# Bank ticks on VectorE, a first pass shared 3:1, and rearranged borders, in a two-layer convolution kernel

## The chip, the cores and the metric

The kernel runs on one core of a Trainium2 chip. The metric is the device time of one execution in microseconds (us). The engines are called as the profile calls them: PE is TensorE's matmul side and PEld its weight loads, DVE is VectorE, ACT is ScalarE, POOL is GpSimd, SP is SyncE, which here only issues DMAs. "L506" is line 506 of the kernel before.

## The reference

The input x is (4, 64, 256, 256) in float32: four images of 64 channels. Two residual layers follow each other, `x = x + layer(groupnorm(x))`, with 32 groups.

```python
# layer 0
h = gelu(conv3x3(gn(x), c1_w) + c1_b)
xa, k = split(conv1x1(h, c2_w) + c2_b)
xs = gelu(conv_3x1(conv_1x3(xa, sh_w), sv_w))          # depthwise
mask = top2(softmax(mean(xs) @ gate_w.T))              # per image, 3 experts
out = xs + sum(e_w3 @ ((e_w2 @ k) * (e_w1 @ xs)) * mask_e)   # ranks 2, 4, 8
x = x + conv1x1(out, proj_w)
# layer 1
g = gn(x)
h = relu(batchnorm(conv3x3(g, quantize(w1)) + b1))
h = batchnorm(conv3x3(h, quantize(w2)) + b2)
x = x + relu(h + g)
```

GroupNorm needs statistics of a whole image before its first convolution, BatchNorm statistics of the whole batch.

## The kernel before

**Stages.** There are six, one after the other. (1) The first pass loads image 0 in 16 chunks of 1 MB (`stats_load`) and takes its statistics. (2) The front works through 64 units of 16 image rows, 16 units to an image: layer 0 up to the gate. Statistics of the next image, and the closing part of layer 0 for the last one (experts, projection, residual, stored to `y_d`), are laced into it. (3) conv1 is layer 1's first convolution; its result goes to `h_d`. (4) The BatchNorm sums are closed (`totals_close`, `bn_affine`), which holds up conv2. (5) conv2 goes over 64 chunks of `h`; the last chunks stay on the chip, 50 go to memory. (6) The end loads `y` (and the 50 `h`) again, applies BatchNorm, both residuals and ReLU, and stores `out`.

**First pass.** DVE takes statistics of 512 elements with `bn_stats` (`stats_group`, L415); ACT takes a piece of 1024 elements with two activations with sums, Identity and Square (`stats_piece`, L444). `stats_parts` gives half of the chunks' elements to each: 32 groups and 16 pieces. `stats_end` joins them: `bn_aggr` over all groups (L475), the sums of ACT's pieces (`stats_sums`, L446), then `combine` (L267–L284), which averages over the channels of a group with two small matmuls. `scale_weights` (L458) multiplies the convolution's weights by the reciprocal deviation, giving `us`; for image 0 in four parts on DVE (L465), for the others on ACT (L467).

**A unit of the front.** The 3x3 convolution is a short Winograd form over rows. POOL makes the transformed inputs: `x_fourths` (L546), `x_seconds` (L554), `v_inner` and `v_outer` (L580–L589), for the next two units. PE multiplies in three groups into two banks `ps_c`: products (1,2), (3,4), then (0,5). ACT copies one half of each bank (`front_copy`, L619), DVE combines (`butterfly_a` to `butterfly_d`, L624–L643), ACT applies GELU (`front_h`, L651). `butterfly_c` (L636, L637) writes into the bank that products (0,5) add to. Then follow the taps of the separable convolutions: `front_taps_a` is 24 matmuls into a bank `ps_a`, `front_taps_b` 8 more into the same bank, for the rows from neighbouring units; ACT (`front_taps_i`, L692) and DVE (`front_taps_h`, L699, L707, L710) finish the horizontal taps, ACT the GELU (L723). This is done twice in a unit, for sub 1 of unit u−2 and for sub 0 of unit u−1.

**Ticks.** Between `front_taps_a` and `front_taps_b` stands `divide` (L497). It writes one column with a memset that waits for the last matmul before it, and the first matmul behind it waits for the memset:

```python
ins = nc.gpsimd.memset(tick, 0.0)
tc.add_manual_dep(ins.ins, last[0].ins.name, finished, reason="bank change")
```

There are two ticks in a unit, at positions 2.2 and 7.2; both are on POOL.

**The order of the work.** It is written out by hand. `at_slot(u, pos, call)` puts a step into slot u; positions under 6 belong to its first half and the others to its second, and steps are emitted sorted by half and position. All five engines keep the order in which instructions are emitted, so an instruction that waits holds up all that stands behind it on its engine. Steps that take several visits, such as `stats_end`, `out_end` and the scaling of layer 1's weights (`weights1_scale`, `weights1`, L253–L255 among its lines), are generators: each visit in the plan runs one of their parts.

**conv1 and conv2.** A convolution over a chunk of 8 rows works on even and odd rows apart. `differences` (L343) and `upper_odd`/`lower_odd` (L359 on ACT, L362 on DVE) prepare the inputs, PE multiplies (L296), DVE writes the result with the sums (L318), and `square` (L382, ACT) takes the sums of squares for BatchNorm. In conv2, `conv2_affine` (L1295) first applies BatchNorm and ReLU to the loaded chunk.

**The end.** For each chunk: load y (L1441), `v = gn2_scale * y + shift` on ACT (L1453), `h = scale * h + v` on DVE (L1454), `h = max(h, 0) + y` on DVE (L1455), store (L1456). SP issues loads and stores in order; nine y loads are issued ahead (AHEAD = 8 and one in the loop), into 3 old tiles and MORE = 6 new ones.

## Time and profile before

| | |
|---|---|
| median of 3 runs | 2990.66 us (2983.44 to 2991.94) |
| the profiled execution | 2990.48 us, its span 2988.7 us |
| PE busy, share of the span | 2351.9 us, 79% |
| DVE | 2440.1 us, 82% |
| ACT | 2024.8 us, 68% |
| POOL | 1682.5 us, 56% |
| bytes moved by DMA | 915.33 MB, 306 GB/s over the span |

The span runs from the first to the last instruction on the chip; 1.8 us of the execution lie outside it. A row of a timeline gives the start and the length in us, the engine, the line, the operation, what it writes and reads, how many follow each other as one row (x3), and in brackets the idle time before it with what ended it. A row of the waits gives the waiting engine and line, the instruction it waited for, the sum in us, how often, and the longest. A row of the stages gives the stretch, its length, the busy time of PE, PEld, DVE, ACT and POOL (with the number of instructions), the granted clock of PE, the busy share of the DMA engines and GB/s. Busy shares are means over stages with different limits, so they say little alone.

### The profile page before, as it was taken

The numbers are of one execution on the slowest core, as the hardware profiler recorded it, in microseconds if no ns is written. First come the engines' busy times: TensorE is split into PE (matmuls) and PEld (weight loads), VectorE is DVE, ScalarE is ACT, GpSimd is POOL, SyncE is SP. The second block draws the span as 40 slices with busy tenths as digits, with TensorE's granted clock in tenths as the row PEclk, the third lists the DMA queues.
The fourth block names the chain that finished last, engine by engine and source line by source line (L and its number), as shares of the span: only waits on it lengthen the run. The fifth ranks groups of instructions, "written<-read, shape, count | busy, mean of one in ns | idle before, by whom it ended". The sixth has DMA issues, their size and how long they took to land.

```text
span 2988.7 us, 52829 instructions
## 1 busy us (share of the span) xinstructions
PE 2351.9 (79%) x21576; PEld 1500.3 (50%) x21576; DVE 2440.1 (82%) x2754; ACT 2024.8 (68%) x2210; POOL 1682.5 (56%) x1283
## 2 busy tenths in 40 slices
PE   1888899999999999989999999989999999100000
PEld 1444445444444555546666667867888888000000
DVE  5678678878878888868988889979999898876665
ACT  6777888778776665567666667968888888432222
POOL 5888888778778888734544546735555565000000
PEclk9999999999999999999999999989999999555555
DMA  8565579999999899849999997747777763899999
GB/s 348 206 237 209 196 270 370 357 350 353 345 336 321 295 320 323 293 181 323 361 345 358 340 337 275 283 164 269 262 266 263 264 234 140 354 420 425 425 424 407
DMA packets 135570, 915.33 MB, mean 306 GB/s; under 512 B 14944, under 2 KB 15712, under 8 KB 40608
## 3 DMA queue, kind: packets, MB, share of 16 engines
q1 hardware_dynamic: 107680, 777.74, 70.1%
q10 hardware_dynamic: 27648, 134.23, 11.3%
q8 instruction: 169, 2.77, 0.4%
q14 instruction: 73, 0.60, 0.1%
HBM read 573.74 MB, written 338.17 MB: 305 GB/s over the span
## 4 chain that ended last, share of the span: by engine, by line
PE 50%; DMA 27%; DVE 10%; POOL 6%; ACT 3%; issue 3%; SPq 0%; ACTq 0%; DVEq 0%; POOLq 0%
PE ps_h L296 19%; PE ps_c L506 8%; PE ps_a L506 6%; PE ps_h2m L296 6%; DMA y<-in_xp 6%; DMA y_d<-y 5%; PE ps_o L506 5%; DMA y_end<-y_d 5%; DMA out<-h 4%; DMA h<-h_d 4%; PE ps_hm L296 3%; POOL x L554 2%; DMA xs_in<-xs_d 2%; DVE y L873 1%; DVE t L707 1%
## 5 line engine op out<-in xcount | busy, mean ns | idle before, releaser
L296 PE MATMUL ps_h<-diff,w_q 128*128 128x512 f32 x3072 | 756.8, 401 | 17.6 <-DVE h L318 17.2
L296 PEld LDWEIGHTS ps_h<-diff,w_q 128*128 128x128 f32 x3072 | 578.9, 190 | 196.1 <-issue 28.8
L506 PE MATMUL ps_c<-v,us 64*64 64x256 f32 x9216 | 538.4, 382 | 28.6 <-DVE ps_c L637 23.8
L343 POOL TENSOR_TENSOR d<-yn 128x1024 f32<-128x1024 f32 x128 | 347.8, 2738 | 305.6 <-DMA yn<-y_d 189.8
L506 PEld LDWEIGHTS ps_c<-v,us 64*64 64x64 f32 x9216 | 359.3, 135 | 180.5 <-DVE ps_c L637 24.2
L506 PE MATMUL ps_a<-h,av 64*64 64x512 f32 x4080 | 388.0, 494 | 55.2 <-DVE t L710 40.1
L343 POOL TENSOR_TENSOR d<-h 128x1024 f32<-128x1024 f32 x127 | 311.9, 2478 | 194.8 <-DVE diff L351 133.3
L318 DVE SCALAR_TENSOR_TENSOR h<-ps_h,scale_w,m 128x1024 f32<-128x1024 f32 x256 | 322.8, 1279 | 73.3 <-PE ps_h L296 53.4
L554 POOL TENSOR_TENSOR x<-x 128x512 f32<-128x512 f32 x256 | 330.0, 1289 | 12.5
L1453 ACT ACTIVATE v<-y_end,shift,gn 128x2048 f32<-128x2048 f32 x64 | 133.8, 2093 | 280.2 <-DMA y_end<-y_d 245.1
L506 PEld LDWEIGHTS ps_a<-h,av 64*64 64x64 f32 x4080 | 153.8, 133 | 331.6 <-issue 203.5
L382 ACT ACTIVATE junk<-h,less_h 128x2048 bf16<-128x2048 f32 (+3 forms) x133 | 255.9, 1924 | 11.1 <-DVE h L318 10.9
L1454 DVE SCALAR_TENSOR_TENSOR h<-h,ss,v 128x2048 f32<-128x2048 f32 x64 | 149.8, 2349 | 121.4 <-ACT v L1453 96.8
L692 ACT ACTIVATE t<-ps_a,tap_bias,m 128x1016 f32<-128x1016 f32 x128 | 153.4, 1199 | 128.7 <-PE ps_a L506 99.7
L873 DVE SCALAR_TENSOR_TENSOR y<-ps_o,ob,y 128x1024 f32<-128x1024 f32 x128 | 163.9, 1280 | 74.8 <-PE ps_o L506 26.8
L723 ACT ACTIVATE xs<-t 128x1024 f32<-128x1024 f32 x128 | 134.8, 1053 | 102.3 <-DVE t L710 88.4
L296 PE MATMUL ps_h2m<-odd,w_q 128*128 128x512 f32 x768 | 193.2, 401 | 8.2 <-DVE odd L362 4.4
L296 PE MATMUL ps_hm<-odd,w_q 128*128 128x512 f32 x768 | 191.4, 398 | 2.8 <-DVE t L710 1.3
L353 DVE SCALAR_TENSOR_TENSOR diff<-d,gn,diff 128x1024 fp32r<-128x1024 f32 x128 | 192.3, 1531 | 0.5 <-ACT diff L346 0.5
L346 ACT ACTIVATE diff<-d 128x1024 fp32r<-128x1024 f32 x128 | 135.1, 1056 | 83.3 <-POOL d L343 82.1
L546 POOL TENSOR_TENSOR x<-x,x 128x512 f32<-128x512 f32 x128 | 160.9, 1280 | 22.2 <-ACT x L540 22.2
L296 PEld LDWEIGHTS ps_h2m<-odd,w_q 128*128 128x128 f32 x768 | 146.3, 191 | 44.5 <-DVE odd L362 5.2
(250 smaller groups left out, 4271.5 us busy)
## 6 DMA issues: line engine op xcount, KB each, us to landing
x<-in_xc SPq DMA_DIRECT2D x64, 1280.0 KB
h<-h_d SPq DMA_DIRECT2D x64, 1152.0 KB
yn<-y_d SPq DMA_DIRECT2D x60, 1152.0 KB
xs_in<-in_xp SPq DMA_DIRECT2D x64, 1024.0 KB
xs_d<-xs ACTq DMA_DIRECT2D x128, 512.0 KB
xs_in<-xs_d SPq DMA_DIRECT2D x64, 1024.0 KB
y<-in_xp SPq DMA_DIRECT2D x64, 1024.0 KB
y_d<-y SPq DMA_DIRECT2D x64, 1024.0 KB
```

The costliest lines, as they stand in the source:

```text
L296: nc.tensor.matmul(ps, wq[w][:, kind, kx, :], t[:, rows, kx : kx + W], start=(j == 0), stop=(j == len(terms) - 1))
L318: nc.vector.scalar_tensor_tensor(h.rearrange("p (e k) w -> p e (k w)", e=2), ps.rearrange("p e k w -> p e (k w)"), w_scale[w], m.unsqueeze ...
L343: engine.tensor_tensor(raw.rearrange("p (g r) w -> p g r w", g=2), *pair, ALU.subtract)
L346: nc.scalar.activation(inner(tiles[0], 4 * n, 4 * n + 4), raw, AF.Copy, scale=scale)
L353: nc.vector.scalar_tensor_tensor(lower, raw, scale, upper.bitcast(F32), ALU.mult, ALU.subtract)
L382: nc.scalar.activation(junk[rows, 0:n], flat(h), AF.Square, bias=less[name][rows], accum_out=total)
L506: last[:] = [nc.tensor.matmul(ps[o, at_out[0] : at_out[1], :], w[i], rhs[i], **flags)]
L546: nc.gpsimd.tensor_tensor(x4[:, j - 1], x_rows(u, j + 2), x4[:, j - 1], ALU.subtract)
L554: nc.gpsimd.tensor_tensor(x[:, r : r + 2], x[:, r + 2 : r + 4], x[:, r : r + 2], ALU.subtract)
L692: nc.scalar.activation(t[:, :, inside], ps[:, :, inside], AF.Identity, bias=tap_bias, scale=sh[:, 1:2])
L873: nc.vector.scalar_tensor_tensor(y, ps.rearrange("p x s w -> p x (s w)"), out_bias[b], y, ALU.add, ALU.add)
L1454: nc.vector.scalar_tensor_tensor(h, h, ss2[:, 0:1], v, ALU.mult, ALU.add)
```

## The change

- `divide` takes the unit. In slots under 16 it writes its tick with a memset on DVE, into a column of its own; elsewhere with POOL as before. These are 29 of the 128 ticks: sub 1 in slots 2 to 15 and sub 0 in slots 1 to 15.
- In the first pass every second chunk, and chunk 14, is split between DVE (two groups) and ACT (one piece); the others, chunk 15 among them, are DVE's whole: 48 groups and 8 pieces. Every 16 groups, `bn_aggr` joins them into a column of `mv_x`, and `combine` gets four columns in place of two. `scale_weights` is on ACT for image 0 too.
- DVE's steps of the weights of layer 1 go from position 6.2 to 7.3, and its second stats groups for image 1 from 6.2 to 7.25, both behind the tick at 7.2.
- Two chain steps go later: one of `stats_end` from (e+2, 6.15) to (e+2, 8.3), the first of `out_end` from (e+1, 4.1) to (e+1, 8.35).
- The square of conv1's last chunk is taken in two halves, the first ahead of the chunk's last output.
- For conv2's first chunk, DVE applies BatchNorm and ReLU to the even rows and the last one, and both first differences are DVE's; ACT's `upper_odd` stands straight behind its odd rows. The odd tiles are allocated ahead of the difference tiles.
- In the end the formula is turned round: DVE `h * inverse + y`, ACT `Relu(gn2_scale * h + shift)`, DVE `h + y`. Part of `inverse` and `shift` is made in conv2, at chunk 8 (`end_scales`, eight one-column operations). The first chunk goes in two halves. MORE is 8, AHEAD is 10, the v tiles are gone, and the order on SP, DVE and ACT is written out.

The diff (lines without a mark are context, "..." stands for lines left out):

```diff
     def stats_group(b, g, k, i):
         if g == 0:
-            st_g[b] = lstat.tile([P, NG // 2, 6], F32, tag="st_x", name=f"st_x{b}", bufs=1)
+            st_g[b] = lstat.tile([P, 3 * NG // 4, 6], F32, tag="st_x", name=f"st_x{b}", bufs=1)
...
+    def stats_join(b, i, n):
+        nc.vector.bn_aggr(mv_x[b][:, 1 + i, :], flat(st_g[b][:, i * n : i * n + n, :]))
+    mv_x = {}
+    PARTS = (4, 2, 1, 1)
...
     def stats_shift(b):
...
-    HALVED = (0, 1)
     def stats_parts(k):
...
     def stats_sums(b, mv):
...
-        n = NCH if b in HALVED else 2 * NCH
+        n = 2 * NCH // PARTS[b]
...
         for a, e in parts:
...
-            if b == 0:
-                nc.vector.tensor_scalar(o, u, gn1[b][:, 1:2], None, ALU.mult)
-            else:
-                nc.scalar.activation(o, u, AF.Copy, scale=gn1[b][:, 1:2])
+            nc.scalar.activation(o, u, AF.Copy, scale=gn1[b][:, 1:2])
+    def stats_open(b):
+        n = PARTS[b]
+        mv_x[b] = stat.tile([P, n, 2], F32, tag=f"mv{n}", name=f"mv_x{b}")
...
     def stats_end(b):
...
-        n = 2 if b in HALVED else 1
-        mv = stat.tile([P, n, 2], F32, tag=f"mv{n}", name=f"mv_x{b}")
-        if b in HALVED:
-            nc.vector.bn_aggr(mv[:, 1, :], flat(st_g.pop(b)))
+        n = PARTS[b]
+        if b > 0:
+            stats_open(b)
+        if n == 2:
+            stats_join(b, 0, NG // 2)
+        mv = mv_x.pop(b)
...
-    tick = column("tick")
+    tick, tick_v = column("tick"), column("tick_v")
...
-    def divide():
-        ins = nc.gpsimd.memset(tick, 0.0)
+    def divide(u):
+        ins = nc.vector.memset(tick_v, 0.0) if u < NCH else nc.gpsimd.memset(tick, 0.0)
...
         if g:
...
-    def conv1_square(b, k):
+    def conv1_square(b, k, part=None):
+        if part is not None:
+            h = h_out[b, k][:, 4 * part : 4 * part + 4, :]
+            square("h1", h, junks[0], squares[b][:, k + 2 * part : k + 2 * part + 1])
+            if part:
+                nc.scalar.dma_start(h1_d[b][:, k * CPAIR : (k + 1) * CPAIR, :], h_out.pop((b, k)))
+            return
...
         if k == 0:
...
+        stats_open(0)
+        groups = pieces = 0
         for k in range(NCH):
...
             if k == 0:
...
-            groups, pieces = stats_parts(k)
-            for group in groups:
-                stats_group(0, *group)
-            for n, at_sum in pieces:
+            both_engines = k % 2 == 1 and k < NCH - 1 or k == NCH - 2
+            for i in range(2 if both_engines else 4):
+                stats_group(0, groups, k, i)
+                groups += 1
+                if groups % (NG // 4) == 0:
+                    stats_join(0, groups // (NG // 4) - 1, NG // 4)
+            if both_engines:
                 for i in range(2):
-                    stats_piece(0, n, i, at_sum)
+                    stats_piece(0, 2 * k + 1, i, pieces)
+                pieces += 1
             if k == 5:
...
             if k == 8:
...
             if 0 <= u - 2 <= last:
...
-                at_slot(u, 2.2, divide)
+                at_slot(u, 2.2, divide, u)
...
             if 0 <= u - 1 <= last:
...
-                at_slot(u, 7.2, divide)
+                at_slot(u, 7.2, divide, u)
...
-        at_slot(3, 6.2, weights1_top)
+        at_slot(3, 7.3, weights1_top)
...
-        at_slot(4, 6.2, next, chain, None)
+        at_slot(4, 7.3, next, chain, None)
         for i, name in enumerate(("w1", "w2")):
...
             for n in range(3):
-                at_slot(7 + 3 * i + n, 6.2, next, chain, None)
+                at_slot(7 + 3 * i + n, 7.3, next, chain, None)
...
     def plan_stats(b):
...
             if k == 0:
...
-            groups, pieces = stats_parts(k) if b in HALVED else ([], [(2 * k, None), (2 * k + 1, None)])
+            groups, pieces = stats_parts(k) if PARTS[b] == 2 else ([], [(2 * k, None), (2 * k + 1, None)])
             for i, (n, at_sum) in enumerate(pieces):
...
             for group in groups:
...
-                at_slot(int(s), 4.1 if s - int(s) < 0.5 else 6.2, stats_group, b, *group)
+                at_slot(int(s), 4.1 if s - int(s) < 0.5 else 7.25, stats_group, b, *group)
...
-        places = (e, 8.3), (e + 1, 1.25), (e + 1, 1.36), (e + 2, 1.25), (e + 2, 1.36), (e + 2, 4.45), (e + 2, 6.15), (e + 3, 1.25), (e + 3, 1.36)
+        places = (e, 8.3), (e + 1, 1.25), (e + 1, 1.36), (e + 2, 1.25), (e + 2, 1.36), (e + 2, 4.45), (e + 2, 8.3), (e + 3, 1.25), (e + 3, 1.36)
...
         for place in places:
...
         if count == NOCT:
...
-            for place in ((e + 1, 4.1), (e + 2, 1.25), (e + 2, 1.36), (e + 3, 1.25), (e + 3, 1.36), (e + 3, 4.45), (e + 3, 8.3)):
+            for place in ((e + 1, 8.35), (e + 2, 1.25), (e + 2, 1.36), (e + 3, 1.25), (e + 3, 1.36), (e + 3, 4.45), (e + 3, 8.3)):
...
     def plan_out_late(b, ns, steps, order, end):
...
-            at(T + 4 + 4 / 3, 13.16, conv1_square, b, k)
+            if (b, k) == (B - 1, NCH - 1):
+                at(T + 4, 12.85, conv1_square, b, k, 0)
+                at(T + 4, 12.92, conv1_square, b, k, 1)
+            else:
+                at(T + 4 + 4 / 3, 13.16, conv1_square, b, k)
...
+    def conv2_affine_vector(i):
+        (even, _), _ = second_rows(h_in[i])
+        for rows in (even, h_in[i][:, CPAIR, :]):
+            nc.vector.tensor_scalar(rows, rows, ss1[:, 0:1], ss1[:, 1:2], ALU.mult, ALU.add)
+            nc.vector.tensor_scalar(rows, rows, 0.0, None, ALU.max)
+        nc.vector.memset(h_in[i][C:P, 0, :], 0.0)
     def conv2_affine(i, part=None):
...
-    diffs2 = [difference_tiles(halves_pool, f"2{i}", 6, CPAIR) for i in range(2)]
-    odds2 = [odd_tiles(halves_pool, f"2{i}", 6, CPAIR) for i in range(2)]
+    diffs2, odds2 = [], []
+    for i in range(2):
+        odds2.append(odd_tiles(halves_pool, f"2{i}", 6, CPAIR))
+        diffs2.append(difference_tiles(halves_pool, f"2{i}", 6, CPAIR))
...
+    inverse = const.tile([P, B], F32, name="inverse")
+    shift = const.tile([P, B], F32, name="shift")
+    def end_scales():
+        for b in range(B):
+            nc.vector.reciprocal(inverse[:, b : b + 1], gn2[b][:, 1:2])
+            nc.vector.tensor_copy(shift[:, b : b + 1], gn2[b][:, 2:3])
...
     def chunk_h2(b, k):
...
         conv2_affine(0, "odd")
+        conv2_affine_vector(0)
+        conv2_differences(0, (nc.vector, nc.vector))
         conv2_upper_odd(0)
-        conv2_affine(0, "rest")
-        conv2_differences(0, (nc.vector, nc.gpsimd))
         conv2_lower_odd(0)
...
         for i in range(n):
+            if i == 8:
+                end_scales()
...
             if i:
...
-    shift = const.tile([P, B], F32, name="shift")
...
-    MORE = 6
+    MORE = 8
...
     def end_load(i):
+        if i >= len(steps):
+            return
...
         if i % (3 + MORE) < 3:
...
+    def end_parts(i):
+        return ((0, CPAIR // 2), (CPAIR // 2, CPAIR)) if i == 0 else ((0, CPAIR),)
+    def end_sum(i):
+        b = steps[i][0]
+        h, y = h2[steps[i]], y_of[i]
+        for a, e in end_parts(i):
+            at_h = h[:, a:e, :]
+            nc.vector.scalar_tensor_tensor(at_h, at_h, inverse[:, b : b + 1], y[:, a:e, :], ALU.mult, ALU.add)
+            nc.scalar.activation(at_h, at_h, AF.Relu, bias=shift[:, b : b + 1], scale=gn2[b][:, 1:2])
+    def end_out(i):
+        b, k = steps[i]
+        h, y = h2.pop((b, k)), y_of.pop(i)
+        for a, e in end_parts(i):
+            at_h = h[:, a:e, :]
+            nc.vector.tensor_tensor(at_h, at_h, y[:, a:e, :], ALU.add)
+            nc.sync.dma_start(io["out"][b, k, :, a * W : e * W], flat(at_h))
     for i in range(AHEAD):
...
-    for b in range(B):
-        nc.vector.tensor_scalar(shift[:, b : b + 1], gn2[b][:, 2:3], ss2[:, 1:2], None, ALU.add)
-    for i, (b, k) in enumerate(steps):
-        if i + AHEAD < len(steps):
+    nc.vector.tensor_scalar(inverse, inverse, ss2[:, 0:1], None, ALU.mult)
+    nc.vector.tensor_scalar(shift, shift, ss2[:, 1:2], None, ALU.add)
+    with tc.manual_schedule(
+        engines={mybir.EngineType.SP, mybir.EngineType.DVE, mybir.EngineType.Activation}
+    ):
+        end_sum(0)
+        for i in range(len(steps)):
+            if i + 1 < len(steps):
+                end_sum(i + 1)
...
-        y, h = y_of.pop(i), h2.pop((b, k))
-        v = end.tile([P, CPAIR, W], F32, tag="v", name=f"v_{b}_{k}")
-        nc.scalar.activation(v, y, AF.Identity, bias=shift[:, b : b + 1], scale=gn2[b][:, 1:2])
-        nc.vector.scalar_tensor_tensor(h, h, ss2[:, 0:1], v, ALU.mult, ALU.add)
-        nc.vector.scalar_tensor_tensor(h, h, 0.0, y, ALU.max, ALU.add)
-        nc.sync.dma_start(io["out"][b, k], flat(h))
-        j = i - 3 + KEEP
-        if i >= 3 and j < len(steps):
-            b2, k2 = steps[j]
-            nc.sync.dma_start(chunk_h2(b2, k2), h2_d[b2][:, k2 * CPAIR : (k2 + 1) * CPAIR, :])
+            end_out(i)
+            j = i - 3 + KEEP
+            if i >= 3 and j < len(steps):
+                b, k = steps[j]
+                nc.sync.dma_start(chunk_h2(b, k), h2_d[b][:, k * CPAIR : (k + 1) * CPAIR, :])
```

## The prediction

> **What bounds the kernel now.** I read the 40 slices first, then a table of stages, then the waits, then the instructions around each changed place.
>
> ```profile
> 65.00:355.00 290.00, 246.56 (x3578) 132.69 (x3582) 213.07 (x289) 219.87 (x302) 250.75 (x235) 0.98 0.56 203
> ...
> 450.00:900.00 450.00, 425.00 (x5921) 219.18 (x5917) 372.73 (x482) 350.40 (x490) 349.49 (x343) 0.99 0.96 351
> ...
> 1987.00:2010.00 23.00, 9.12 (x25) 6.72 (x24) 14.03 (x29) 13.33 (x14) 7.51 (x9) 0.56 0.27 103
> 2010.00:2548.00 538.00, 537.68 (x2289) 430.86 (x2287) 492.79 (x537) 448.80 (x377) 306.99 (x132) 1.00 0.65 238
> 2548.00:2989.00 441.00, 0.80 (x4) 0.65 (x4) 298.64 (x151) 135.36 (x67) 0.00 (x0) 0.51 0.99 414
> ```
>
> The columns are the stretch, its length, the busy time of PE, PEld, DVE, ACT and POOL, the granted clock, the DMA share and GB/s. Different resources limit the stages: image 0 (first row) is a loop in which no engine is full and DMA is half idle; images 1 and 2 are at the DMA limit; conv2 is PE alone; the end is DMA alone. The first pass (0 to 65 us) is DMA at 1.01 and 425 GB/s from 8 to 56 us, and then a serial tail. What counts is therefore serial time at 50–70, in image 0's loop, at 1987–2004 and at 2550–2565.
>
> The waits view puts GpSimd's tick high. This is how such a view can mislead:
>
> ```profile
> POOL tick L499 <- PE ps_a L506: 163.9, 79, 11.3
> ...
> PE ps_a L506 <- POOL tick L499: 13.7, 25, 2.4
> ```
>
> GpSimd waits 163.9 us in its ticks, over all images; TensorE waits only 13.7 for them. Who waits for GpSimd's other work decides, so I read one unit of image 0 in the timeline, engine by engine:
>
> ```profile
> 162.00 0.10 POOL L499 MEMSET tick<- 128x1 f32 x1 [2.05 <-PE ps_a L506]
> ...
> 162.15 0.66 PE L506 MATMUL ps_a<-h,av 64*64 64x256 f32 x8 [0.25 <-POOL tick L499]
> ...
> 167.42 2.38 PE L506 MATMUL ps_a<-h,av 64*64 64x512 f32 x24 [1.22 <-DVE t L710]
> ```
>
> A unit is 17.7 us (ps_c begins at 119.0, 136.7, 154.4, 172.1). GpSimd has 12 × 1.286 = 15.4 us of work in it and idles 2.05, all at tick 1; its v tiles are ready about 14 us ahead of TensorE. It has slack. The loop closes through TensorE, ACT L692, DVE L699/L707/L710, TensorE.
>
> [...]DVE's L343 (1024 wide, two inputs) is 1.23 us, its L362 3.37 us beside a POOL L343; L465 took 6.28 us for four small scalings beside POOL L546. [...]no tick on DVE is in the trace. [...]the trace's end is at 422–428.
>
> **First pass.**
>
> ```profile
> 54.03 0.19 DVE L450 TENSOR_REDUCE st_sum<-st_acc 128x2 f32<-128x32 f32 x1 [4.73 <-ACT xs_in L444]
> ...
> 61.42 6.28 DVE L465 TENSOR_SCALAR us<-u_raw,gn 128x384 f32<-128x384 f32 x4
> ...
> 65.04 4.29 PE L506 MATMUL ps_c<-v,us 64*64 64x256 f32 x48 [4.45 <-DVE us L465]
> ```
>
> (The L465 row is the timeline of this stretch taken over 57 to 68 us.) ACT's pieces (16 × 2 before) run to 53.9 and hold DVE. After, 8 × 2, the last on chunk 14, which lands near 48: ACT ends near 50.7. Chunk 15 lands near 50.7 by the DMA's records, so DVE does its four groups (4 × 0.61 = 2.46) and a join: bn_aggr of 192 elements is 1.02, of 384 (image 2) 1.88, so 96 is about 0.59. Sums 51.4, groups 53.9, join 54.5, against 58.24: −3.7. Then ScalarE scales us: [...]DVE's first took about 3.5 beside GpSimd. That is another −3.0 for the first matmul (65.04 to about 58.2). But e of unit 0 (ACT L563) waits for GpSimd's L546 and L554 (2.47 + 5.41 us), ahead of the copies of ps_c; this chain starts when the mean is known, 3.7 earlier, and is shortened only a little. I take −5.6 for the start, bounds −3.7 and −6.8.
>
> **Image 0's 29 ticks** (14 tick 1, 15 tick 2; 0.10 us on GpSimd; DVE's MEMSET L370, 34 wide, is 0.09, so equal). Gain: TensorE's tick wait beyond 0.25 vanishes: 2.06 at 100.72, 0.78 at 316.37, 0.97 at 335.29, together −3.1 beyond that floor; the usual wait shrinks by perhaps 0.07 in some units, −0.5. Cost: tick 1 waits on DVE behind L632 for the last of 24 matmuls; queued behind it are L636/L637, for which the (0,5) part of ps_c waits, then a stats group, L699, L707, L710. In the seven units whose last gap is 1.22 (one is shown above) I count 0.18 each: +1.3; in the others (0.92) DVE had room. Tick 2 has the weights step and the stats group moved behind it (7.3, 7.25). The stats group has 1.93 us before L764: hidden. The 768-wide weights steps (4.8 us, at 221.03 and 274.25, where TensorE's ps_a ends near 222.3 and 275.5) slip 1.45 each, twice, and two smaller steps 0.2 each: +3.3. Sum: −3.1 − 0.5 + 1.3 + 3.3 = +1.0, bounds −4 (the two costs are hidden) and +8 (tick 1 costs 0.4 in every unit). A larger gain needs GpSimd to be the pace.
>
> **Chain steps moved later** (reciprocal of image 1's and 2's statistics, bn_aggr of out_end): the 1.88 us bn_aggr leaves the full butterfly stretch at 750, but that stretch is DMA's. −0.5, bounds −2 and +1. The steps issue no DMA; what follows them is GpSimd's L482, placed a unit later and already waiting some 6 us for VectorE per image with GpSimd's x work behind it; GpSimd's slack of 2 us a unit takes a longer wait, and +1 is what it costs if it doesn't.
>
> **conv1's last chunk and conv2's first.**
>
> ```profile
> 1991.34 0.19 DVE L390 TENSOR_REDUCE sum_h<-squares 128x1 f32<-128x34 f32 x1 [2.17 <-ACT junk L382]
> ...
> 2004.12 4.21 PE L296 MATMUL ps_h2m<-odd,w_q 128*128 128x512 f32 x9 [4.44 <-DVE odd L362]
> ```
>
> The square in halves does its first half before the last out, so L390 waits for 1.15 instead of 2.2: −1.1. ss at 1994.4; the even rows now on DVE, beside ACT's odd rows: two passes of 1024 elements at no more than L707's 1.28 for 1020, two over 256 and a memset, taken as 0.3 each like GpSimd's memset (0.31), so at most 3.5, and I take 3.2: 1997.6. Two differences at 1.23, now with no GpSimd reader beside them, 2000.1; lower odd, of the same width, 2001.3; PE 2001.4 against 2004.12: −2.8, bounds −1 and −4. The x3 matmuls before it cover nothing.
>
> **End.**
>
> ```profile
> 2560.00:2565.00 5.00, 0.00 (x0) 0.00 (x0) 5.00 (x3) 3.99 (x2) 0.00 (x0) 0.50 0.17 70
> ```
>
> ```profile
> 2564.26 0.34 SPq L1456 DMA_DIRECT2D out<-h  x1
> ```
>
> The stages view gives the hole, the timeline the first store. DMA is 1.01 from 2550, drops to 0.17 at 2560–2565 since nine loads are spent and no out is ready, then is full to 2985. The first out needs shift (2554.55 + 0.58), ACT 2.1, and two DVE steps of 4.6 and 4.5 for pairs. After: 11 loads before the first out (+2 × 1.05 MB / 0.4245 = 4.9 us of cover), and out(0) in halves, each 1.2 + 1.1 + 1.2 from 2555.3 on, first about 2561. The hole closes. But the sixth load lies over junk_2 and waits for the last square on ScalarE (2550.4; before, loads went from 2547.22), and five queue behind it on SP. From 2551.4 the 173 transfers that are left (59 y, 64 out, 50 h) × 1.0486 MB / 0.4245 = 427.3 us end at 2978.7, against 2983.7 for the last packets before: −5, of which I take −4.7; bounds 0 (the hole is only moved ahead to 2547–2551) and −7. The order on SP is otherwise unchanged, and TensorE's wholly; the formula is 2 DVE + 1 ACT operations per chunk as before, at the mean 2.35 and 2.09 us of these rows, under the 7.4 us that the DMA needs for its three transfers. The 8 tiny end_scales steps (8 × 0.16 = 1.3 us at chunk 8) hide in DVE's slack (493 of 538); with no cover they cost 1.3.
>
> **Sum:** −5.6 + 1.0 − 0.5 − 2.8 − 4.7 = −12.6. The profiled execution is 2990.48 (span 2988.7 + 1.8 outside it); the median is 2990.66, so no correction: 2977.9, stated as 2978.
>
> **Rivals.**
> - GpSimd is the pace of image 0. For: 2.05 us idle in each unit at tick 1. Then about 14 units × 2.05 = −29 more: 2949. Against: v lies 14 us ahead, and TensorE waits for DVE and ACT in that loop. Chance 0.05.
> - The end's hole only moves ahead (its loads blocked by the last square) and the weights steps cost in full: −5.6 + 3.3 − 2.8 − 1 = −6, 2984. For: the sixth load's wait. Chance 0.22.
> - Slower: the DVE tick blocks the DVE queue. While it waits for TensorE nothing behind it runs: L636/L637, stats, L699. Slack in the loop is 0.9–1.2 us per unit. If it is spent, each of 29 ticks costs its whole wait; from about 0.45 us each the 13 are gone, at 0.9 it is +26 − 13: 3004. For: DVE is 213 of 290 busy and in the loop. Against: TensorE ends ps_a just about when DVE reaches the tick (161.9 and 161.87). Chance 0.07.
> - The forecast itself: 0.66.
>
> A measurement tells about 0.3%, 9 us, from no change: faster is under 2981.7. Of the forecast's cases about 0.62 lie there, plus 0.05 of the first rival and 0.03 of the second: 0.70; slower 0.07; same 0.23. Range 2964 to 2987: the low end adds the bounds of start (−1.2), ticks (−5), chain (−1.5), conv2 (−1.2) and end (−2.3), −11, and a little of rival one; the high end takes in the second rival with 3 us about it.
>
> **What would show it.** Start: first ps_c matmul near 58–60, not 65. Ticks: unit cycle still about 17.7, GpSimd's idle moved elsewhere. conv2: nine ps_h2m matmuls near 2001 less the shift so far. End: DMA share 1.0 with no slice under 0.9 after the last square. Wrong if the unit cycle changes by over 0.5 us either way, or TensorE waits for DVE L637 grow.

## The result, and the profile after

The changed kernel takes 2971.39 us (median of 11 runs, 2963.18 to 2985.03), the kernel before 2983.44 us (median of 11 runs beside them, 2978.37 to 2994.01). The ratio is 0.9959, with a 95% interval of 0.9941 to 0.9978: 12.2 us less, between 6.6 and 17.6. The forecast was 12.6 us less. It was counted from the 2990.66 us of the three runs of before shown above; eleven runs have a lower median, and the 6.6 us between the forecast 2978 us and the measured 2971.4 us come from there. The profiled execution of the changed kernel took 2970.49 us, its span is 2968.7 us: 20.0 us under the profiled execution of before, more than the runs show. Where the 8 us between the two come from is told below, since a reader who compares just these two profiles explains too much.

Line numbers in the rows below are those of the kernel that the row is from. The table of stages of the changed kernel, with the stretches moved so that they begin about where the same work begins:

```profile
57.00:347.00 290.00, 247.55 (x3586) 137.55 (x3590) 211.56 (x315) 221.90 (x307) 254.38 (x210) 0.98 0.59 214
442.00:892.00 450.00, 426.54 (x5963) 218.22 (x5957) 376.20 (x486) 353.25 (x498) 353.43 (x348) 1.00 0.97 353
1967.00:1990.00 23.00, 12.74 (x43) 9.49 (x42) 19.25 (x36) 12.67 (x14) 6.02 (x7) 0.70 0.28 103
1990.00:2524.00 534.00, 533.02 (x2272) 427.06 (x2270) 491.51 (x544) 446.94 (x376) 304.40 (x131) 1.00 0.67 241
2524.00:2969.00 445.00, 0.74 (x4) 0.59 (x4) 293.32 (x151) 135.85 (x68) 0.00 (x0) 0.51 1.00 408
```

Every stage has the limit that it had. TensorE's 12.74 us of work between conv1 and conv2, where before had 9.12 in a stretch of the same length, is the shorter border. The last row is the surprise: the DMA engines are busy at a share of 1.00 (0.99 before) and yet move 408 GB/s, not 414.

GpSimd waits less for TensorE in its ticks, since 29 of them are gone. TensorE waited 13.7 us for ticks (25 waits) and waits 5.3 us now: 3.7 us for VectorE's (15 waits) and 1.6 us for GpSimd's (6 waits, not in the rows below).

```profile
POOL tick L506 <- PE ps_a L513: 129.0, 66, 9.8
...
DVE tick_v L506 <- PE ps_a L513: 3.9, 3, 1.3
PE ps_a L513 <- DVE tick_v L506: 3.7, 15, 0.6
```

The first pass in the timeline (the sums on VectorE; the weights on ScalarE; the first matmul of the convolution):

```profile
49.64 0.17 DVE L454 TENSOR_REDUCE st_sum<-st_acc 128x2 f32<-128x16 f32 x1 [1.21 <-ACT xs_in L448]
...
52.82 0.59 DVE L418 BATCH_NORM_AGGREGATE mv_x<-st_x 128x2 f32<-128x96 f32 x1
...
56.52 1.81 ACT L468 ACTIVATE us<-u_raw,gn 128x384 f32<-128x384 f32 x4 [0.23 <-DVE gn L284]
...
57.28 4.57 PE L513 MATMUL ps_c<-v,us 64*64 64x256 f32 x48 [1.52 <-ACT us L468]
```

VectorE waits 1.21 us for ScalarE's last piece where it waited 4.73, and the convolution starts at 57.28, not at 65.04. The border between conv1 and conv2:

```profile
1970.09 0.19 DVE L390 TENSOR_REDUCE sum_h<-squares 128x1 f32<-128x34 f32 x1 [0.86 <-ACT junk L382]
...
1978.99 1.22 DVE L362 TENSOR_TENSOR odd<-h,odd 128x1024 fp32r<-128x1024 f32 x1
...
1980.26 4.21 PE L296 MATMUL ps_h2m<-odd,w_q 128*128 128x512 f32 x9 [2.12 <-DVE odd L362]
```

From conv1's last output (1986.74 before, 1966.80 now) to the nine matmuls it was 17.4 us and is 13.5.

### The profile page after: what moved, and what is told of

Read it like the earlier page. It is cut to its first block, busy times and chain, and to the rows that moved or that the text cites. A ratio compares the mean times of both kernels' runs of the same rounds, so it can differ in the third digit from the quotient of the medians.

```text
span 2968.7 us, 52737 instructions
## 1 busy us (share of the span) xinstructions
PE 2348.6 (79%) x21576; PEld 1504.2 (51%) x21576; DVE 2444.9 (82%) x2811; ACT 2008.8 (68%) x2183; POOL 1676.3 (56%) x1252
## 3 DMA queue, kind: packets, MB, share of 16 engines
q10 hardware_dynamic: 27648, 134.23, 11.3%
## 4 chain that ended last, share of the span: by engine, by line
PE 51%; DMA 28%; DVE 12%; ACT 3%; issue 2%; POOL 2%; SPq 0%; ACTq 0%; DVEq 0%; POOLq 0%
PE ps_h L296 20%; PE ps_c L513 9%; DMA y<-in_xp 7%; PE ps_a L513 6%; PE ps_h2m L296 6%; DMA y_d<-y 5%; DMA y_end<-y_d 5%; PE ps_o L513 4%; DMA h<-h_d 4%; DMA out<-h 4%; PE ps_hm L296 4%; DVE t L714 1%; DVE t L717 1%; DMA yn<-y_d 1%; DMA xs_in<-in_xp 1%
## 5 line engine op out<-in xcount | busy, mean ns | idle before, releaser
L296 PE MATMUL ps_h<-diff,w_q 128*128 128x512 f32 x3072 | 756.5, 401 | 14.6 <-DVE h L318 14.2
L343 POOL TENSOR_TENSOR d<-yn 128x1024 f32<-128x1024 f32 x128 | 346.2, 2724 | 305.9 <-DMA yn<-y_d 194.8
L343 POOL TENSOR_TENSOR d<-h 128x1024 f32<-128x1024 f32 x126 | 308.1, 2467 | 205.8 <-DVE diff L351 136.9
L561 POOL TENSOR_TENSOR x<-x 128x512 f32<-128x512 f32 x256 | 329.2, 1286 | 12.8
L1497 ACT ACTIVATE h<-h,shift,gn 128x2048 f32<-128x2048 f32 (+1 forms) x65 | 134.3, 2067 | 282.1 <-DVE h L1496 279.9
L382 ACT ACTIVATE junk<-h,less_h 128x2048 bf16<-128x2048 f32 (+3 forms) x134 | 256.3, 1912 | 13.6 <-DVE h L318 13.5
L1496 DVE SCALAR_TENSOR_TENSOR h<-h,inverse,y_end 128x2048 f32<-128x2048 f32 (+1 forms) x65 | 150.6, 2318 | 128.0 <-DMA y_end<-y_d 128.0
L353 DVE SCALAR_TENSOR_TENSOR diff<-d,gn,diff 128x1024 fp32r<-128x1024 f32 x128 | 200.8, 1598 | 0.8 <-ACT diff L346 0.5
L553 POOL TENSOR_TENSOR x<-x,x 128x512 f32<-128x512 f32 x128 | 160.7, 1278 | 34.4 <-ACT x L547 34.3
L717 DVE SCALAR_TENSOR_TENSOR t<-ps_a,m,t 128x1020 f32<-128x1020 f32 x128 | 163.9, 1281 | 4.6
```

The lines of the kernel that those rows point to most:

```text
L296: nc.tensor.matmul(ps, wq[w][:, kind, kx, :], t[:, rows, kx : kx + W], start=(j == 0), stop=(j == len(terms) - 1))
L343: engine.tensor_tensor(raw.rearrange("p (g r) w -> p g r w", g=2), *pair, ALU.subtract)
L353: nc.vector.scalar_tensor_tensor(lower, raw, scale, upper.bitcast(F32), ALU.mult, ALU.subtract)
L382: nc.scalar.activation(junk[rows, 0:n], flat(h), AF.Square, bias=less[name][rows], accum_out=total)
L553: nc.gpsimd.tensor_tensor(x4[:, j - 1], x_rows(u, j + 2), x4[:, j - 1], ALU.subtract)
L561: nc.gpsimd.tensor_tensor(x[:, r : r + 2], x[:, r + 2 : r + 4], x[:, r : r + 2], ALU.subtract)
```

## The spread, and how the experiments are read

The ratio of an experiment's runs has an interval of about 5 us to each side. Parts worth 1 to 7 us don't show in it. But image 0 is not paced by DMA, and once it is under way two executions of the same instructions keep their distance to some hundredths of a microsecond (0.04 us at most from 103 to 299 us, in the run with 1.3 us more on GpSimd below). Their starts differ: of before's instructions, four traces reach the first `front_taps_h` at 102.0 to 102.7 us, and of the changed kernel's, three traces end image 0 8.0, 8.4 and 8.9 us ahead of before. A difference of under 1 us between two traces at the end of image 0 means something only when it grows on the way. So I take the place of one operation in each unit (the first of `front_taps_h`) and of some landmarks from the traces. In the table, the first row has the times of before in us and the others what each kernel's trace has more or less. "First ps_c" is the first matmul of the convolution, "image 0 done" and "1027 us" are the first `front_taps_h` of image 1 and of image 3, "nine ps_h2m" are the matmuls shown above:

| | first ps_c | image 0 done | 1027 us | conv1's last output | nine ps_h2m | conv2's last output | span |
|---|---|---|---|---|---|---|---|
| before | 65.0 | 391.9 | 1027.2 | 1986.7 | 2004.1 | 2547.9 | 2988.7 |
| changed | −7.8 | −8.4 | −17.0 | −19.9 | −23.9 | −24.5 | −20.0 |
| ticks alone | −0.6 | −1.7 | −9.7 | −10.0 | −10.0 | −10.2 | +3.8 |
| first pass alone | −7.8 | −7.2 | −12.7 | −14.5 | −14.5 | −15.3 | −12.4 |
| end alone | −0.8 | −0.2 | +7.9 | +7.9 | +7.9 | +7.6 | +8.3 |
| borders alone | −0.6 | −0.7 | −4.7 | −7.7 | −11.3 | −12.5 | −11.3 |
| GpSimd +1.3 us | −0.5 | +0.4 | −5.5 | −5.0 | −5.2 | −5.2 | −5.7 |

The kernel with the new end alone has the instructions of before until deep into conv2, and it lies 7.9 us behind at 1027; the one with more work on GpSimd in image 0 has them from slot 16 on, and gains 5.9 between image 0's end and 1027. So the DMA-bound stage of one and the same code moves by 6 to 8 us either way. The changed kernel's profile gained 8.6 us there. Two more traces with its instructions in this stage, from experiments below that change only conv2 or the end, gained 6.3 us and lost 0.8 us; the kernel with the ticks alone gained 8.0. The 8.6 us are inside that spread and are no effect of the change that these runs could show.

## Experiments: the parts alone

**The ticks, with the weights steps and the stats groups behind tick 2**, on the kernel before:

```diff
+        ins = nc.vector.memset(tick_v, 0.0) if u < NCH else nc.gpsimd.memset(tick, 0.0)
...
-        at_slot(3, 6.2, weights1_top)
+        at_slot(3, 7.3, weights1_top)
...
-                at_slot(int(s), 4.1 if s - int(s) < 0.5 else 6.2, stats_group, b, *group)
+                at_slot(int(s), 4.1 if s - int(s) < 0.5 else 7.25, stats_group, b, *group)
```

> The kernel before with the ticks of image 0 on VectorE, and the weights steps and the stats groups of image 1 moved behind the tick at 7.2; nothing else of the change. Theory A (ticks are hidden by slack): image 0 ends within 2 us of before (its unit cycle stays near 17.7 us), whole time -2 to +3 us. Theory B (GpSimd's tick is the pace of image 0): the unit cycle falls by 1 to 2 us, image 0 ends 15 to 29 us earlier. Theory C (the tick on VectorE blocks its queue): the cycle grows by 0.5 us or more, image 0 ends 8 us or more later. For the stretch from 780 to 1010 us, where the changed kernel gained 9 us more: if the ticks or the moved groups caused it, it shows here; if it is the spread of single executions, it does not.

Measured: ratio 0.9988 (0.9969 to 1.0008). Image 0 ends 1.7 us earlier. At the first matmul of `front_taps_a`, the last place ahead of a tick, it is 0.6 us ahead already, so about 1.1 us are the ticks and the moves. Unit by unit: −2.4 at the first tick (the 0.6 us of the start included), +0.6 by 156 us, nothing until 209, +1.0 at 227, where the 768-wide weights steps now stand behind the tick, −0.9 at 318, and nothing else. A tick on VectorE:

```profile
220.65 0.69 DVE L415 BATCH_NORM_STATS2 st_x<-xs_in 128x6 f32<-128x512 f32 x1 [1.26 <-issue]
220.67 0.06 DVE L499 MEMSET tick_v<- 128x1 f32 x1
...
221.85 1.38 DVE L253 TENSOR_SCALAR mset<-mset,inv_w 128x768 f32<-128x768 f32 x1
```

VectorE stands still for 1.26 us ahead of this tick, with the weights steps queued behind it; TensorE goes on at 222.39 without a wait. It stands still like this, 1.2 to 1.3 us, at 14 of the 15 ticks at 7.2 and longer at the first. From 156 us on it shows only in this unit, where the weights steps come next: `front_taps_h` loses 1.0 us of its lead. Theory A holds; B and C fall for image 0.

**The first pass**, on the kernel before:

```diff
+            both_engines = k % 2 == 1 and k < NCH - 1 or k == NCH - 2
+            for i in range(2 if both_engines else 4):
+                stats_group(0, groups, k, i)
...
-            if b == 0:
-                nc.vector.tensor_scalar(o, u, gn1[b][:, 1:2], None, ALU.mult)
```

> The kernel before with the first pass shared 3:1 and the first weights scaled on ScalarE; nothing else. Theory A: first ps_c matmul near 57.3 us instead of 65.0, and the lead of 6 to 8 us is kept to the end of image 0 and to the end of the kernel: whole time -5 to -8 us. Rival: the lead is used up by GpSimd's x work in the first units (its v tiles are late), then image 0 ends less than 3 us earlier.

Measured: ratio 0.9988 (0.9970 to 1.0005), 20 runs. First matmul at 57.22, 7.8 us ahead; in every unit from 138 us to the end of image 0 the trace is 7.10 to 7.19 us ahead, so from there on nothing of the lead is used up. In the whole time the interval, −9 to +1.5 us, holds the 7 and doesn't show it; that the lead lasts to the end of the kernel is not shown by this run.

**The end**, on the kernel before:

```diff
-    MORE = 6
+    MORE = 8
...
-        v = end.tile([P, CPAIR, W], F32, tag="v", name=f"v_{b}_{k}")
+    def end_sum(i):
...
+            if i == 8:
+                end_scales()
```

> The kernel before with the end of the changed one (formula turned round, first chunk in halves, 11 loads ahead, order written out, end_scales in conv2); nothing else. From the last output of conv2 to the end of the span, before took 439.6 us and the changed kernel 444.0. Theory A (closing the hole in the DMA's work is worth 4 to 5 us, and the slow transfers in the changed kernel's end, 400 GB/s for 140 us, are the chance of one execution): about 435 us. Theory B (the new order of loads and stores makes the transfers themselves slower): 441 to 446 us, with 395 to 405 GB/s in the first 150 us of the end.

Measured: ratio 1.0001 (0.9983 to 1.0019). From the last output of conv2 to the end 440.3 us: between the two theories. The stretches from 12 us after that output on:

```profile
2568.00:2573.00 5.00, 0.00 (x0) 0.00 (x0) 5.00 (x4) 2.56 (x2) 0.00 (x0) 0.50 1.02 421
2573.00:2582.00 9.00, 0.00 (x0) 0.00 (x0) 9.00 (x5) 4.26 (x3) 0.00 (x0) 0.50 1.00 370
2582.00:2702.00 120.00, 0.00 (x0) 0.00 (x0) 102.84 (x47) 47.78 (x24) 0.00 (x0) 0.50 1.01 414
2702.00:2822.00 120.00, 0.00 (x0) 0.00 (x0) 71.42 (x32) 32.71 (x16) 0.00 (x0) 0.50 1.01 414
```

The first is where before had its hole of 0.17; it is full now. So the hole is closed, and the end is no shorter. I come back to this.

**The borders**, on the kernel before:

```diff
+                at(T + 4, 12.85, conv1_square, b, k, 0)
+                at(T + 4, 12.92, conv1_square, b, k, 1)
...
+        conv2_affine_vector(0)
+        conv2_differences(0, (nc.vector, nc.vector))
```

> The kernel before with the last conv1 chunk's square in two halves and the first conv2 chunk's even rows and both differences on VectorE; nothing else. Theory A: from the last output of conv1 to the nine ps_h2m matmuls 17.4 us before, 13.5 after, and 3 to 4 us off the whole time. Its end is that of the kernel before and gives another sample of the 439.6 us from the last output of conv2 to the end.

Measured: ratio 0.9989 (0.9975 to 1.0004). 13.8 us from conv1's last output to the nine matmuls, 17.4 before. As theory A has it at this place; in the whole time the interval, −7.5 to +1.2 us, holds its 3 to 4 us and doesn't show them.

## Experiments: the ticks

Two kernels load GpSimd on purpose, ahead of tick 1; the second has `range(4)`:

```diff
+    def more_work():
+        for _ in range(2):
+            nc.gpsimd.tensor_tensor(zeros, zeros, zeros, ALU.mult)
+        for u in range(2, NCH):
+            at_slot(u, 2.15, more_work)
```

> The kernel before with two more GpSimd multiplications of 258 elements (about 0.65 us each, over a tile of zeros) directly ahead of tick 1 in slots 2 to 15. Theory A (GpSimd has 2 us of slack in each unit of image 0): tick 1 fires when it did, image 0 is within 1.5 us of before. Theory B (GpSimd is the pace of image 0): each unit is 1.3 us longer, image 0 ends 18 us later.

> The same with four more multiplications, about 2.6 us a unit, which is more than the 2.05 us of idle time. Theory A: the cover is gone; about 0.5 us a unit shows, image 0 ends 5 to 10 us later. Theory B: 2.6 us a unit, 36 us later.

Tick 1 of the unit that the prediction showed, in the first and then in the second kernel:

```profile
159.89 1.31 POOL L1066 TENSOR_TENSOR zeros<-zeros 128x258 f32<-128x258 f32 x2
161.99 0.10 POOL L499 MEMSET tick<- 128x1 f32 x1 [0.78 <-PE ps_a L506]
```

```profile
161.19 2.69 POOL L1066 TENSOR_TENSOR zeros<-zeros 128x258 f32<-128x258 f32 x4
163.82 0.10 POOL L499 MEMSET tick<- 128x1 f32 x1
```

With 1.31 us more in each unit the idle time falls from 2.05 to 0.78 and the tick fires when it did. From 103 to 299 us this trace and that of before differ by 0.04 us at most, and image 0 ends 0.4 us later. With 2.69 us the idle time is gone, TensorE waits 0.80 instead of 0.25 us at this tick, and image 0 ends 9.8 us later: 0.7 us a unit. This is what slack looks like: nothing until it is used up, and then what goes over it. GpSimd isn't the pace of image 0. That rival is out.

**All 128 ticks on VectorE, nothing else moved**, on the kernel before:

```diff
-        ins = nc.gpsimd.memset(tick, 0.0)
+        ins = nc.vector.memset(tick, 0.0)
```

> The kernel before with all 128 ticks on VectorE, the steps of the weights and the stats groups left where they were. Theory A (what matters is whether VectorE has slack where the tick stands): image 0 as in the run with its ticks alone; images 1 to 3 within 5 us of before, since DMA paces them until 900 us and TensorE after. Theory C (the tick blocks VectorE's queue): the stretch from 900 us on, where VectorE is 88% busy, grows by 0.3 us or more a unit, 5 us or more over 20 units. The end, which is that of before, gives one more sample.

Measured, in one run (2980.16 us): from 900 to 1275 us VectorE is busy 88% of the time, and the trace gains on before there (3.2 us ahead at 909, 6.4 at 1065), and from 1065 to 1271 us it keeps that distance within 0.04 us. The loss that theory C names isn't there. But the case that it needs isn't there either: between 900 and 1275 us VectorE never stands still for more than 0.14 us ahead of a tick, since it comes to each when TensorE's matmul is done. A VectorE that waits while it is nearly full was not tried. Image 0 is another matter: it ends 2.6 us later, 4.3 us behind the kernel with its ticks alone. VectorE and TensorE around 222 us:

```profile
219.63 1.22 DVE L253 TENSOR_SCALAR mset<-mset,inv_w 128x768 f32<-128x768 f32 x1
...
225.09 0.06 DVE L499 MEMSET tick<- 128x1 f32 x1
```

```profile
225.22 1.13 PE L506 MATMUL ps_a<-h,av 64*64 64x256 f32 x8 [2.44 <-DVE tick L499]
```

The weights steps at 6.2 stand ahead of the tick and hold it until 225.09; TensorE waits 2.44 us. A wait of this kind is what moving them to 7.3 avoids.

**The steps back at 6.2 in the changed kernel:**

```diff
-        at_slot(3, 7.3, weights1_top)
+        at_slot(3, 6.2, weights1_top)
...
-                at_slot(7 + 3 * i + n, 7.3, next, chain, None)
+                at_slot(7 + 3 * i + n, 6.2, next, chain, None)
...
-                at_slot(int(s), 4.1 if s - int(s) < 0.5 else 7.25, stats_group, b, *group)
+                at_slot(int(s), 4.1 if s - int(s) < 0.5 else 6.2, stats_group, b, *group)
```

> The changed kernel with the weights steps and the stats groups of image 1 at 6.2 again, ahead of tick 2. Theory A1 (behind the tick they are delayed, which I had put at 3.3 us): image 0 ends up to 3 us earlier than in the changed kernel. Theory A2 (ahead of it they delay the tick, which now stands on their engine; the run with all ticks on VectorE and these steps at 6.2 ended image 0 4.3 us behind the run with them moved): image 0 ends about 4 us later. Its end gives one more sample of the new order: 441 to 445 us.

Measured, in one run (2973.18 us): image 0 ends at the same time as in the changed kernel (−8.3 against −8.4), having been 1.2 us ahead of it at its first unit. So the moves are worth 1.2 us here, not 4: the sign of A2, a third of its size. As with all ticks on VectorE, the loss falls on the unit around before's 227 us: this kernel loses 2.2 us on before there and in the half unit behind it, the changed kernel 1.0.

**All ticks on GpSimd in the changed kernel:**

```diff
-        ins = nc.vector.memset(tick_v, 0.0) if u < NCH else nc.gpsimd.memset(tick, 0.0)
+        ins = nc.gpsimd.memset(tick, 0.0)
```

> The changed kernel with all ticks on GpSimd. Theory A (VectorE's ticks are worth 1.7 us in image 0, by the run with them alone): image 0 ends 1 to 2 us later than in the changed kernel, whole time within 2 us of it. Theory B (they are what the change lives by): 10 us or more later. One more sample of the new end: if the new order slows the transfers, 445 us as in the changed kernel's own execution; if chance did, 441.

Measured: ratio 0.9937 (0.9912 to 0.9962), against 0.9959 (0.9941 to 0.9978) of the changed kernel. The two ratios come from different sets of runs of before. Image 0 ends at −7.75, 0.65 us later than with VectorE's ticks; at the first matmul of `front_taps_a` the two traces were within 0.03 us of each other, so this isn't a difference of their starts. The part that heads the change is worth about 0.65 us; in the whole time it can't be seen. That is less than the 1 to 2 us of theory A, and theory B is out.

## Experiments: two details

**The first image's weights on VectorE again**, in the changed kernel:

```diff
+            if b == 0:
+                nc.vector.tensor_scalar(o, u, gn1[b][:, 1:2], None, ALU.mult)
```

> The changed kernel with the first image's weights scaled on VectorE again. Theory A[...]: they take 5 to 6.5 us again beside GpSimd's L553, and the first ps_c matmul starts near 60.2 us instead of 57.3. Rival (the width alone costs it): they take under 2 us in sum, and the start is as in the changed kernel. Its end is the new one and gives another sample of 444 us from the last output of conv2.

```profile
56.84 6.28 DVE L469 TENSOR_SCALAR us<-u_raw,gn 128x384 f32<-128x384 f32 x4
```

They take 6.28 us once more, ScalarE's took 1.81. The first matmul starts at 60.45, 3.2 us later, and image 0 ends 4.0 us later. The width alone doesn't set the length: apart, the two operations of 384 elements take 3.46 and 1.42 us, the two of 192 take 1.32 and 0.31 (before: 3.47, 1.42, 1.32 and 0.31). The first three end at 60.30, 61.64 and 62.89, each just after a moment at which GpSimd passes from one operation to its next (60.16, 61.51 and 62.85); ahead of the first of these moments three GpSimd operations had followed each other without a gap. That the operations beside them set their length fits these moments; more than that isn't shown.

**The second difference on GpSimd again**, in the changed kernel:

```diff
-        conv2_differences(0, (nc.vector, nc.vector))
+        conv2_differences(0, (nc.vector, nc.gpsimd))
```

> The changed kernel with the second difference of conv2's first chunk on GpSimd again. Theory A[...]: VectorE's lower odd takes 2.4 us or more instead of 1.22, and the nine ps_h2m matmuls start 0 to 2 us later than the 13.5 us after conv1's last output. Rival (GpSimd beside it costs nothing): VectorE has one operation less, and they start 1.2 us earlier. One more sample of the new end.

```profile
1979.41 2.36 POOL L343 TENSOR_TENSOR d<-h 128x1024 f32<-128x1024 f32 x1 [8.63 <-DVE h L1319]
...
1979.76 3.09 DVE L343 TENSOR_TENSOR d<-h 128x1024 f32<-128x1024 f32 x1
1982.77 1.21 DVE L362 TENSOR_TENSOR odd<-h,odd 128x1024 fp32r<-128x1024 f32 x1
```

GpSimd's difference starts first, and VectorE's own, which takes 1.18 alone (2.36 for two in the changed kernel), takes 3.09: it ends about when GpSimd's does, plus its own length. I had put the wait on L362; it falls on the operation that meets GpSimd's, and L362 comes after. The nine matmuls start 14.3 us after conv1's last output, 0.8 later than in the changed kernel. One VectorE operation less, and still later.

## Where the end's gain went

**The end of before in the changed kernel:**

```diff
-    MORE = 8
+    MORE = 6
...
-    def end_sum(i):
+        v = end.tile([P, CPAIR, W], F32, tag="v", name=f"v_{b}_{k}")
```

> The changed kernel with the end of the kernel before. Theory A (the new end saves the DMA 3.9 us of idle time and transfers run at the same rate on average): idle time of the DMA engines from 35 us ahead of the last output of conv2 to the end 23.6 us, against 19.7 in the new end, and whole time about 4 us above the changed kernel's. Theory B (the new order slows transfers by 1%): whole time as in the changed kernel.

Measured: 2971.12 us (7 runs), ratio 0.9940 (0.9918 to 0.9961), against 0.9959 (0.9941 to 0.9978) with the new end. The new end buys nothing that shows; the 4 us of theory A lie inside these intervals.

There are now eight traces with the old end and six with the new one. In each I take the time from the last output of conv2 (the row that reads its sum) to the end, the time in which no DMA packet is under way from 35 us ahead of that output to 25 us after it, and the rate from there on:

| | old end (8 traces) | new end (6 traces) |
|---|---|---|
| idle of the DMA, us | 21.6 to 24.3, mean 23.3 | 18.7 to 20.3, mean 19.6 |
| MB moved in the same 60 us | 12.3 to 12.6 | 14.2 |
| rate after that, without the last 5 us, GB/s | 409.0 to 423.7, mean 419.9 | 404.8 to 420.7, mean 415.6 |
| last output to the end, us | 439.1 to 453.5, mean 443.1 | 439.5 to 453.1, mean 443.0 |

The first two rows are the mechanism that was predicted, and it is there in every trace: the DMA idles 3.7 us less and is 1.8 MB ahead. The fourth row is where it should arrive, and it can't be seen there. The third stands between: 1% less in the rate over some 400 us is 4 us. But the ranges of the rate overlap nearly wholly, with the DMA at a share of 1.00 to 1.01 in all. The runs are spread over several chips, and that isn't it: three traces of the old end from one chip have 409.0, 420.8 and 423.2. Three stretches of 120 us of the old end, in the kernel with the ticks alone, and then of the new end, in the one with GpSimd's difference:

```profile
2564.00:2684.00 120.00, 0.00 (x0) 0.00 (x0) 96.89 (x43) 40.81 (x20) 0.00 (x0) 0.50 1.01 402
2684.00:2804.00 120.00, 0.00 (x0) 0.00 (x0) 71.74 (x31) 32.44 (x16) 0.00 (x0) 0.50 1.01 406
2804.00:2924.00 120.00, 0.00 (x0) 0.00 (x0) 72.19 (x32) 33.27 (x16) 0.00 (x0) 0.50 1.01 412
```

```profile
2554.00:2674.00 120.00, 0.00 (x0) 0.00 (x0) 101.44 (x46) 47.61 (x23) 0.00 (x0) 0.50 1.01 407
2674.00:2794.00 120.00, 0.00 (x0) 0.00 (x0) 71.27 (x32) 33.14 (x16) 0.00 (x0) 0.50 1.01 403
2794.00:2914.00 120.00, 0.00 (x0) 0.00 (x0) 68.70 (x31) 31.76 (x16) 0.00 (x0) 0.50 1.01 402
```

Both kinds have executions at 402 to 412, and both have some at 421 to 426. Whether the new order also costs about 1% of the rate, or the six draws happened to be worse, these traces can't tell: the spread between executions (14 us in the end's length) is nearly four times the effect, and the difference of the two means is uncertain by some 5 us either way. Open.

## Why the prediction was right, point by point

The time (2971.4 against 2978, within 2964 to 2987) and its sign were right, and the difference (12.2 us against 12.6) too. The terms were less right than their sum. The sizes below are from landmarks in the traces; in the whole time no part shows alone, and the four kernels with one part each are 3.6, 3.6 and 3.3 us faster and 0.3 us slower (ticks, first pass, borders, end), each to within 4 to 6 us.

- **First pass, −5.6: the mechanism right, the size off by 1.5.** Measured −7.1 at image 0's end, just outside its bounds (−3.7 to −6.8). The join came 4.8 us earlier and not 3.7, since ScalarE was done at 49.6, not 50.7; the weights on ScalarE gave 2.9 as predicted (3.0). What ScalarE would need for 384 elements was an estimate of mine that no trace of before shows (there it scales 1152 at once, in 1.24 us); it took 0.61. What failed was the hold-back that I took for ScalarE's e behind GpSimd's L553 and L561: it cost 0.6 at the most.
- **Ticks, +1.0: wrong sign, small.** Measured about −1.1 for ticks and moves alone. TensorE's shorter waits gave 2.1 us (1.2 by 156 us, 0.9 at 318), not 3.6. Two costs failed. The +1.3 for tick 1 wasn't there: no unit from 156 to 209 us got longer. The +3.3 for the weights steps was +1.0 at 227 us and nothing at 275 us or at the two smaller steps. I had treated the move as a delay of those steps only. Ahead of a tick on their own engine they can hold TensorE, for 2.44 us where all ticks were on VectorE. By the kernel that takes them back, ticks on VectorE are worth 0.65 us in the changed kernel.
- **Rival "GpSimd is the pace"**: the idle time of 2.05 us in each unit was read as slack, and the kernels with more work show that it is, to within the size that was predicted for it.
- **Rival "slower"**: VectorE's queue does stand still at a tick (1.26 us in the row above), in nearly every unit of image 0, and the slack hides it but for the 1.0 us at 227 us. At 88% busy it cost nothing because no tick found VectorE early.
- **Borders, −2.8: right, the size off by 1.1.** Measured −3.9. The halved square gave 1.3 and not 1.1, and VectorE's part took 2.6 us and not 3.2: its tensor_scalar on 1024 elements took 0.81 and 0.69, well under the 1.28 of an operation with two inputs which I had used as a ceiling.
- **End, −4.7: not shown.** The sixth load waited for the last square as predicted (SP issued it at 2526.10, right after that square ended at 2526.08), and the hole closed. The second rival feared that the hole only moves ahead of that load. A gap of 5.6 us is there, but before had one of 5.2 us at that place too. But "the 173 transfers that are left at 0.4245 MB/us" took the rate of one execution as a constant. It is 409 to 424 between executions of the same end, and the 3.7 us of saved idle time don't appear in the length of the end; whether chance covers them stays open. The sum also set its end against "2983.7 for the last packets before", and the last packet of that trace ended at 2987.3, so its own −5 would have been −8.6. As far as these runs go, the end is nearer to the second rival, which had it at −1.
- **Chain steps, −0.5:** not tried apart. They lie in the DMA-bound stage, where the spread of 8 us hides them.

Without the end, the parts as measured are −7.1 − 1.1 − 3.9 = −12.1, which is the whole difference; with its interval of 6.6 to 17.6 us it would hold 4 us more from the end too. If the end gave nothing, that the predicted sum fits is luck: the end was then put 4.7 us too high, and first pass, ticks and borders together 4.7 too low.

One term in each of the two parts that paid came from work that no longer runs on VectorE beside GpSimd's: the weights (2.9 us of the first pass) and the second difference (0.8 us of the border). Both long times came back when that was undone: 6.28 us for the four scalings, as before, where ScalarE took 1.81, and 3.09 us for a difference that takes 1.18 alone. The rest of the two parts is work shared out between VectorE and ScalarE. The rate of one trace is no rate to plan with: the end ran at 404.8 to 423.7 GB/s in the fourteen.

## What to carry to other kernels

A long idle row of an engine that waits for another says nothing of what its removal brings; put work into the gap and see whether anything moves. When a waiting instruction goes to another engine, look first at what stands ahead of it on that engine's queue (here the weights steps, 2.44 us of TensorE's time). And in a stage that only drains DMA, compare idle time and bytes, not lengths: one trace's GB/s is one draw (409.0, 420.8 and 423.2 here, with one end on one chip).

## What was not expected of the hardware

- The same transfers, with the DMA engines busy at a share of 1.01, ran at anything from 402 to 426 GB/s over 120 us, from one execution to the next.
- Image 0, where the DMA share is 0.56, repeats itself: two executions kept their distance within 0.04 us over 200 us, though their starts had differed by half a microsecond.
- A VectorE difference that met GpSimd's took about the rest of GpSimd's operation and then its own length: 3.09 us for 1.18 alone, beside 2.36 on GpSimd, which had started 0.35 earlier. A VectorE `tensor_scalar` of 384 elements took 3.46 us, to the end of three GpSimd operations in a row, where the next of 384 took 1.42. Not every operation is long beside GpSimd's: before, three of 768 elements at 221 us took 1.51 to 1.70 us with GpSimd busy beside them nearly all the time, and VectorE's L343 took 1.23 us from 1999.56, with GpSimd's L343 beside it from 1999.73.
